# A second Strassen level in three products of a cross-attention and FFN kernel

## The chip, the cores and the metric

The kernel runs on one NeuronCore of a Trainium2 chip. The metric is the device time of one execution in microseconds (us). TensorE (PE in the profile) does the matmuls, VectorE (DVE) and ScalarE (ACT) the elementwise work, GpSimd (POOL) a few small steps, and SyncE (SP) issues all the transfers (DMAs) from one queue. A weight load of TensorE is a separate instruction, shown as the row PEld.

## The reference, cut to what matters

```
x = x + matmul(fake_quant(layernorm(x)), fake_quant(ctx))     # x: 2 x 1024 x 2048, ctx: 2 x 2048 x 2048
y = layernorm(x)
w = top-2 softmax weights of y @ W_router.T                   # 8 experts
lora = einsum(y @ lora_A, lora_B, w) * 2                      # rank 16 per expert
x = x + y @ W_base.T + b_base + lora                          # W_base: 2048 x 2048
```

All of it is in float32. `fake_quant` rounds to 256 levels, so the first GEMM is exact with float16 operands. The second GEMM, `y @ W_base.T`, needs more than float16: each operand is split into a high and a low float16 part, and a product takes three matmuls (low by high, high by low, high by high).

## The kernel before

The two batches run one after the other. For each, the first GEMM (`gemm1` for batch 0, `gemm1w` for batch 1), a second layer norm (`ln2`), the operands of the second GEMM (`y_prep`) and the second GEMM itself (`g2`) follow.

**Second GEMM.** It is done with the Winograd form of Strassen's method: 7 block products in place of 8. Rows are taken in NP = 4 pairs `p` of 128-row tiles, so a 2 by 2 block of the left matrix is (tile 2p, tile 2p+1) by (first, second half of the 2048 depth). `y_prep` makes seven left operands for each pair, `a11, a12, a22, s1, s2, s3, s4`, each by normalizing, adding or subtracting halves, splitting into high and low float16, and transposing by a DMA (`emit`, lines 1007 to 1023). They stay in SBUF. The output columns are two halves `cp` of 1024, one in each pass `f` = 0, 1. A pass has four groups `grp` (the table `GROUPS`), with the right operands made by `w_step` for each `k` of the HK = 8 blocks of the depth: loads of `W`, subtractions on DVE, a scaled high part (`hi`, ACT or DVE), the low part (`lo`, DVE, line 1211). A product is HK x NP x 3 = 96 matmuls of 512 columns (line 1406). At the last `k` of a group the LoRA matmuls (line 1423) and the evacuations follow: `x += scale * PSUM` on DVE (line 1435), 512 columns at a time. `put` stores finished output tiles.

Batch 0 in pass 1 stores ready right operands to DRAM (`store_w`, tiles `made`), and batch 1 in its pass 0, which has the same columns, loads them. The residual `x` tiles are stored (`spill`) before the second GEMM and loaded again for their pass (`reload`, tiles `xr`).

**Memory.** Nearly all of SBUF is one pool `u` of 49 slots, and PSUM has 8 banks. Bytes of the quantized values go through three buffers `byte`, which are handed out in a fixed rotation.

**Order.** Nothing is issued in the order of the code. Every step is a task with modelled durations, its reads and writes, and a priority (the time `t` at which TensorE is due to need it). `Plan.order` is a list scheduler with a model of the engines, of the DMA queue and of the slots. It fixes the order of every engine and of the SP queue when the kernel is built. On the chip each queue then runs strictly in that order: an instruction that waits holds all that is queued behind it on its engine.

## Time and profile before

| what | value |
|---|---|
| median of 3 runs | 910.81 us (910.04 to 912.2) |
| profiled execution, own time | 910.92 us |
| its span, first to last instruction | 909.1 us |
| PE busy, matmuls | 896.0 us, 4542 |
| DVE busy | 708.0 us |
| ACT busy | 388.7 us |
| DMA queue of SP | 240.23 MB, 86.8% of 16 engines' span |

Engine rows of the profile give busy time and its share of the span. The span is also cut into 40 slices of 22.7 us, each with one digit, the busy share in tenths. A group of instructions is listed with its source line, its operation, what it writes and reads, its count, its busy time, the mean ns of one, and the idle time of the engine just ahead of them with the releaser. Matmuls are pipelined: one of 512 columns is shown with 379 ns, but the next one starts after some 216 ns, so their pace is read from the distance of starts.

### The profile page before, as it was taken

Reading aid. Unit: us, or ns where it says so; the run is one execution under the profiler, and the core shown is the slowest. Engines: PE = TensorE matmul, PEld = TensorE weight load, DVE = VectorE, ACT = ScalarE, POOL = GpSimd, SP = SyncE. Lnnn points to the kernel's source line nnn. Section 1 sums busy time; section 2 is a strip of 40 time slices with the busy share of each in tenths; the row PEclk is TensorE's granted clock in tenths of the full one; section 3 lists DMA queues with packets and bytes.
Section 4 is the critical chain, followed back from the end, with each engine's and each line's share of the span. In section 5 each row is a group of like instructions: output and inputs, shape, how many; then the busy total and the mean of one; then the engine's idle time right before and its main releaser. Section 6 shows DMA issues by size and latency. Waiting matters only on the chain.

```text
span 909.1 us, 12499 instructions
## 1 busy us (share of the span) xinstructions
PE 896.0 (99%) x4542; PEld 432.4 (48%) x4542; DVE 708.0 (78%) x1305; ACT 388.7 (43%) x445; POOL 47.4 (5%) x199
## 2 busy tenths in 40 slices
PE   8899999999999999999999999999999999999998
PEld 6344446474444444444444444556444444444443
DVE  8989999999499966999889979999543363899131
ACT  4875976525144221323686776754100021324000
POOL 1014000000000000002540000000000000000000
PEclk9999999999999999999999999999999999999999
DMA  9999999998999999999999748999994169883021
GB/s 327 387 386 278 348 285 225 245 265 226 255 362 325 314 395 406 380 369 345 301 343 323 243 170 235 228 169 222 308 283 109 50 224 371 288 337 134 6 93 46
DMA packets 223917, 241.02 MB, mean 265 GB/s; under 512 B 146032, under 2 KB 158320, under 8 KB 223856
## 3 DMA queue, kind: packets, MB, share of 16 engines
q1 hardware_dynamic: 223856, 240.23, 86.8%
q8 instruction: 35, 0.57, 0.3%
q14 instruction: 26, 0.21, 0.1%
HBM read 163.65 MB, written 41.94 MB: 226 GB/s over the span
## 4 chain that ended last, share of the span: by engine, by line
PE 85%; DVE 9%; DMA 3%; issue 1%; SPq 1%; ACT 0%; DVEq 0%; ACTq 0%
PE X L1406 34%; PE Y L1406 27%; PE g L829 11%; PE gX L949 3%; PE ph L1067 3%; PE gY L949 2%; DVE x L858 2%; PE X L1423 2%; PE Y L1423 2%; PE ph L1071 1%; DMA x<-in_x_dram 1%; DVE byte L455 1%; DMA bs<-in_cx_dram 1%; DVE sm L478 1%; DVE bt L920 1%
## 5 line engine op out<-in xcount | busy, mean ns | idle before, releaser
L1406 PEld LDWEIGHTS <-y_s 128*128 128x128 f16 x1536 | 150.3, 98 | 181.0
L1406 PE MATMUL Y<-w,y_s 128*128 128x512 f16 x768 | 206.6, 379 | 0.0
L1406 PE MATMUL X<-w,y_s 128*128 128x512 f16 x768 | 206.3, 379 | 0.0
L1406 PE MATMUL X<-w,y_a 128*128 128x512 f16 x768 | 189.1, 379 | 0.2 <-DVE w L1211 0.2
L1406 PEld LDWEIGHTS <-y_a 128*128 128x128 f16 x1152 | 112.1, 98 | 132.6 <-issue 0.5
L829 PE MATMUL g<-b,at 128*128 128x512 f16 x512 | 112.5, 379 | 4.7 <-DVE b L469 3.6
L1406 PE MATMUL Y<-w,y_a 128*128 128x512 f16 x384 | 103.2, 379 | 0.0
L444 ACT ACTIVATE w<-wb,gW 128x1024 f16<-128x1024 f32 (+1 forms) x46 | 50.0, 1091 | 111.1 <-DVE wb L1282 32.9
L1435 DVE SCALAR_TENSOR_TENSOR xr<-X,uW,xr 128x512 f32<-128x512 f32 x64 | 46.8, 746 | 46.9 <-PE X L1423 25.7
L829 PEld LDWEIGHTS <-at 128*128 128x128 f16 x512 | 49.7, 98 | 64.3 <-issue 4.2
L1435 DVE SCALAR_TENSOR_TENSOR xr<-Y,uW,xr 128x512 f32<-128x512 f32 x42 | 31.1, 745 | 53.8 <-PE Y L1423 53.8
L1211 DVE SCALAR_TENSOR_TENSOR w<-wb,gW,w 128x1024 f16<-128x1024 f32 (+1 forms) x48 | 57.0, 1194 | 6.0 <-ACT w L444 5.9
L444 ACT ACTIVATE byte<-bs,sc,rec 128x1024 uint8<-128x1024 f32 x40 | 48.3, 1236 | 13.5 <-DMA bs<-in_cx_dram 8.6
L444 ACT ACTIVATE w<-wt,gW 128x1024 f16<-128x1024 f32 x15 | 17.0, 1145 | 78.5 <-DVE wt L1258 38.7
L478 DVE BATCH_NORM_STATS2 sm<-x 128x6 f32<-128x512 f32 x64 | 40.9, 683 | 5.5 <-ACT q L444 4.2
L877 ACT ACTIVATE byte<-x,sm 128x1024 uint8<-128x1024 f32 x32 | 36.4, 1139 | 10.4 <-DVE x L858 6.8
L444 ACT ACTIVATE nat_s<-yt_a 128x1024 f16<-128x1024 f32 x31 | 31.9, 1049 | 20.0 <-DVE yt_a L1026 14.7
L949 PEld LDWEIGHTS <-at 128*128 128x128 f16 x256 | 25.0, 98 | 29.8
L1026 DVE TENSOR_TENSOR yt_a<-yt_a,yt_a 128x1024 f32<-128x1024 f32 x32 | 38.7, 1221 | 0.0
L1018 DVE TENSOR_TENSOR nat_s<-yt_a,nat_s 128x1024 f16<-128x1024 f32 x32 | 38.2, 1224 | 0.0
L1067 PE MATMUL ph<-ar,y_a 128*128 128x272 f16 x192 | 35.7, 279 | 0.0
L1071 PE MATMUL ph<-ar,y_a 128*128 128x136 f16 x192 | 34.6, 223 | 0.0
(196 smaller groups left out, 1107.1 us busy)
## 6 DMA issues: line engine op xcount, KB each, us to landing
bs<-in_cx_dram SPq DMA_DIRECT2D x64, 512.0 KB, 10.5
wt<-in_wT_dram SPq DMA_DIRECT2D x64, 512.0 KB, 7.4
wn<-in_wT_dram SPq DMA_DIRECT2D x32, 512.0 KB, 9.1
x<-in_x_dram SPq DMA_DIRECT2D x30, 512.0 KB, 8.4
spill<-x SPq DMA_DIRECT2D x28, 512.0 KB, 4.4
xr<-spill SPq DMA_DIRECT2D x28, 512.0 KB, 8.5
wb<-in_wT_dram SPq DMA_DIRECT2D x24, 512.0 KB, 7.8
out_dram<-xr SPq DMA_DIRECT2D x24, 512.0 KB, 4.0
```

The lines of the kernel that those rows point to most:

```text
L444: nc.scalar.activation(o, i, AF.Copy if c is None else AF.Identity, scale=1.0 if a is None else a, bias=0.0 if c is None else c,)
L478: nc.vector.bn_stats(st[:, 2 * h + c], b.ap()[:, c * C : (c + 1) * C])
L829: nc.tensor.matmul(ps.ap(), aT.ap()[:, k, :], S["b", c, k // 4].ap()[:, k % 4, :], start=k == 0, stop=k == KT - 1,)
L877: nc.scalar.activation(low(sq), xb.ap(), AF.Square, bias=a[:, 22 + j : 23 + j], accum_out=a[:, 24 + 2 * j + h : 25 + 2 * j + h],)
L949: nc.tensor.matmul(ps.ap(), a()[:, 4 * h + k, :], w.ap()[:, k, :], start=fresh and h + k == 0, stop=h == 1 and k == 3, skip_group_check=True,)
L1018: lambda: nc.vector.tensor_tensor(n.ap()[:, 1], t.ap(), n.ap()[:, 0], ALU.subtract),
L1026: add("DVE", 1.22, lambda: nc.vector.tensor_tensor(dst.ap(), a.ap(), c.ap(), op), r=[a, c], w=[dst])
L1067: nc.tensor.matmul(ph.ap()[:, : 2 * AR], y[half].ap()[:, 0, k, :], ar[:, kr, :], start=kk == 0, stop=False,)
L1071: nc.tensor.matmul(ph.ap()[:, AR : 2 * AR], y[half].ap()[:, 1, k, :], ar[:, kr, :AR], start=False, stop=kk == KT - 1,)
L1211: lambda: nc.vector.scalar_tensor_tensor(w.ap()[:, 1, lo:up], src(), g, w.ap()[:, 0, lo:up], ALU.mult, ALU.subtract),
L1406: nc.tensor.matmul(ps.ap(), y.ap()[:, a, k, :], w.ap()[:, q, j * C : (j + 1) * C], start=k == 0 and fresh and i == 0, stop=k == HK - 1 and ...
L1435: nc.vector.scalar_tensor_tensor(xs, ps.ap(), uW[:, cp : cp + 1], xs, ALU.mult, ALU.add)
```

## The change

Three of the block products of batch 1 get a second Strassen level: `a22` in pass 0, `a22` and `a12` in pass 1 (`LEVEL2`). Such a product pairs the row pairs again (`q` = 0, 1 holds `p` = 2q and 2q+1) and cuts depth and columns in half again, so it becomes seven products of 4 blocks of depth, with 256 columns for each matmul (`quarters`). Two of its left operands come from `y_quarters`, which loads the spilled `x` again, normalizes it, combines quarters, and splits and transposes the results `q31` and `q24`; the third operand is the whole one that exists already.

For that, two more `x` tiles are spilled, and the `a12` operands of batch 1 are stored to DRAM in pass 0 (`y_out`) and loaded in pass 1 (`y_in`). A sum of blocks of `W` in float32 goes through DRAM too (`store_t4`): in batch 0, pass 0, group 1 stores its sum of three blocks, and group 3 loads it with the one block that is missing and subtracts once, where it loaded two whole rows and subtracted twice before; it stores the result, which is the right operand of `a22`, over it. Pass 1 stores that of the other column half in its group 2. Batch 1 loads these in quarters. The byte buffers are handed out as they come free, not in rotation, and the planner's time for a transpose on TensorE (`TMM`) is 0.08 in place of 0.12 us.

```
-TMM = 0.12
+TMM = 0.08
+MM2 = 0.1095
+LEVEL2 = {(0, 0): (), (0, 1): (), (1, 0): ("a22",), (1, 1): ("a22", "a12")}
+YOUT = ((), ("a12",))
+YQ = ((), ("a22", "a12"))
...
     def byte(name):
         def make():
-            ring = rings["byte"]
-            ring.append(ring.pop(0))
-            return ring[-1]
+            return rings["byte"].pop(0)
...
+    def y_out(S, b, p, o, when):
+        y = S["y", p, o]
+        d = Buf("dram", lambda: dram.tile([P, 2, HK, P], F16, name=f"yout_{o}_{b}_{p}"))
+        load(d, d.ap, y.ap, HD * 4, [d], r=[y], store=True, cap=when)
+        S["yout", p, o] = d
+
+    def y_in(S, b, p, o):
+        y = buf("u", [P, 2, HK, P], F16, f"yin_{o}_{b}_{p}")
+        d = S["yout", p, o]
+        load(y, y.ap, d.ap, HD * 4, [y], r=[d], far=YFAR)
+        S["y", p, o] = y
+
+    def y_quarters(S, b, q, o):
+        yt = []
+        j = int(o[1]) - 1
+        for p in (2 * q, 2 * q + 1):
+            s = S["s2", p]
+            d = S["spill", 2 * p + j, 1]
+            t = buf("u", [P, HD], F32, f"yq_{o}_{b}_{p}")
+            load(t, t.ap, d.ap, HD * 4, [t], r=[d])
+            affine(t.ap, t.ap, HD, [(s, [j])], [t], scale=lambda s=s: s.ap()[:, 10 + j : 11 + j],
+                   bias=lambda s=s: s.ap()[:, 12 + j : 13 + j])
+            yt.append(t)
...
+        comb(lambda: up(c), lambda: lo(c), lambda: up(c), ALU.add, [], c)
+        comb(lambda: lo(c), lambda: lo(a), lambda: lo(c), ALU.subtract, [a], c)
+        comb(lambda: lo(a), lambda: up(c), lambda: lo(a), ALU.subtract, [c], a)
+        comb(lambda: up(a), lambda: up(a), lambda: lo(a), ALU.subtract, [], a)
+        y_emit(S, b, 2 * q, o + "q31", c)
+        y_emit(S, b, 2 * q, o + "q24", a)
...
-                if h == b and p >= SPILL0:
+                if h == b and p >= SPILL0 and f"a{1 + i % 2}2" not in YQ[b]:
                     continue
...
+    def store_t4(k, cp, s, cap):
+        if cp not in whole_t4:
+            whole_t4[cp] = Buf(
+                "dram", lambda: dram.tile([P, HK, C], F32, name=f"t4_{cp}"), HK)
+        d = whole_t4[cp]
+        load(d, lambda: d.ap()[:, k], lambda: s.ap()[:, :C], C * 4, [(d, [k])], r=[s],
+             store=True, cap=cap)
...
+            elif not b:
+                s = buf("u", [P, HD], F32, f"wb_{n}")
+                d = whole_t4[cp]
...
+                load(s, lambda: s.ap()[:, C:], lambda: d.ap()[:, k], C * 4, [s], r=[(d, [k])], far=WFAR)
...
+        if grp == 2 and "a22" in LEVEL2[b, f]:
+            s = buf("u", [P, 2, C], F32, f"ws_{n}")
...
+    QUARTERS = (
+        ("b11", "", 0, 0), ("t1", "q31", 4, 0), ("t2", "q24", 0, 0), ("b22", "q24", 4, 0),
+        ("t3", "q31", 0, 0), ("b21", "", 4, 0), ("t4", "", 4, 1),
+    )
+
+    def quarters(S, b, f, cp, t, o):
+        g = gW[:, cp : cp + 1]
+        H2 = C // 2
+        raw, made_w = {}, {}
+        for h, n in ((0, 0), (0, 1), (1, 1), (1, 0)):
+            s = buf("u", [P, 4, H2], F32, f"wq{o}_{cp}_{h}{n}")
...
+            load(s, s.ap, src, HD * 4, [s], r=r, slow=SLOW_Q, far=WFAR)
+            raw[h, n] = s
...
+        split("b11", b11)
+        comb(t3, b22, b12)
+        comb(b12, b12, b11)
+        split("t1", b12)
+        t2 = b11
+        comb(t2, b22, b12)
+        split("t2", t2)
+        split("b22", b22)
+        split("t3", t3)
+        split("b21", b21)
+        comb(b21, b21, t2)
+        split("t4", b21)
...
+        for name, op, k0, side in QUARTERS:
+            w = made_w[name]
+            for q in range(NP // 2):
+                y = S["y", 2 * q + side, o + op]
...
+                def mm(ps=ps, col=col, fresh=fresh, y=y, w=w, k0=k0):
+                    for k in range(4):
+                        for i, (a, h) in enumerate(((1, 0), (0, 1), (0, 0))):
+                            nc.tensor.matmul(
+                                ps.ap()[:, col : col + H2], y.ap()[:, a, k0 + k, :],
+                                w.ap()[:, h, k * H2 : (k + 1) * H2],
...
+                add("PE", 12 * MM2, mm, r=[y, w], w=[ps], prio=t)
+                t += 12 * MM2
+                xP, xQ = top[2 * q], top[2 * q + 1]
+                if name == "b11":
+                    ev(ps, 0, H2, xP, 0)
+                elif name == "t1":
+                    ev(ps, 0, H2, xP, H2)
+                    ev(ps, 0, H2, xQ, H2)
...
+        for o in YQ[b]:
+            for q in range(NP // 2):
+                y_quarters(S, b, q, o)
...
+            for o in YOUT[b]:
+                for p in range(NP):
+                    if f:
+                        y_in(S, b, p, o)
+                    else:
+                        y_out(S, b, p, o, t + YO_T + 3.0 * p)
...
+                if grp == 3 and LEVEL2[b, f]:
+                    for o in LEVEL2[b, f]:
+                        t = quarters(S, b, f, cp, t, o)
+                    continue
...
         for task in order:
             task.fn(task.eng) if len(task.durs) > 1 else task.fn()
+            for b in task.bufs:
+                uses[b] -= 1
+                if b.tag in rings and not uses[b]:
+                    rings[b.tag].append(b.tile)
```

`split` is the high part (ACT or DVE) and the low part (DVE) of a right operand of 1024 columns; `comb` of `quarters` is one subtraction of 1024 columns on DVE; `ev` is an evacuation as before, of 256 or 512 columns. `y_emit` is `emit` of `y_prep` as a function of its own. The LoRA matmuls of the three products stay the same in number.

## The prediction

> **What bounds the kernel now.** I read the engine shares first, then the slices, the chain, the groups of instructions, the timeline, and at last windows of 25 us around the places that the change touches.
>
> ```profile
> span 909.1 us, 12499 instructions
> PE 896.0 (99%) x4542; PEld 432.4 (48%) x4542; DVE 708.0 (78%) x1305; ACT 388.7 (43%) x445; POOL 47.4 (5%) x199
> PE   8899999999999999999999999999999999999998
> DVE  8989999999499966999889979999543363899131
> ACT  4875976525144221323686776754100021324000
> PEclk9999999999999999999999999999999999999999
> DMA  9999999998999999999999748999994169883021
> PE 85%; DVE 9%; DMA 3%; issue 1%; SPq 1%; ACT 0%; DVEq 0%; ACTq 0%
> ```
>
> TensorE is the bound at full clock. DVE and the DMA queue are near full for the first two thirds, but from slice 29 on (659 us, the second GEMM of batch 1) DVE, ACT and DMA have room, except DVE in slices 34 to 36.
>
> ```profile
> L1406 PE MATMUL X<-w,y_a 128*128 128x512 f16 x768 | 189.1, 379 | 0.2 <-DVE w L1211 0.2
> L1435 DVE SCALAR_TENSOR_TENSOR xr<-X,uW,xr 128x512 f32<-128x512 f32 x64 | 46.8, 746 | 46.9 <-PE X L1423 25.7
> 882.56 18.78 PE X L1406 x87
> 7.82 5.62 PE L771 MATMUL warm<-ones 128*128 128x256 f16 x50
> 13.28 0.82 PE L780 MATMUL warm<-ones 128*128 128x256 f16 x6
> ```
>
> The second GEMM's matmuls wait for nothing (0.2 us idle in 768). The chain gives their pace: 18.78 / 87 = 215.9 ns for 512 columns, not the 379 ns shown. The timeline gives it for 256 columns: 50 warm-up matmuls, each with its own weight load, take 13.28 - 7.82 = 5.46 us, 109.2 ns each.
>
> ```profile
> 16.40:40.07 23.67, 17.43 (x116) 8.97 (x117) 22.66 (x69) 18.18 (x17) 0.00 (x0) 1.00 1.05 389
> 575.00:600.00 25.00, 25.00 (x127) 11.99 (x126) 22.34 (x65) 19.50 (x22) 0.00 (x0) 1.00 1.01 203
> 600.00:625.00 25.00, 25.00 (x194) 16.29 (x193) 25.00 (x27) 10.68 (x14) 0.00 (x0) 1.00 1.11 185
> 700.00:725.00 25.00, 25.00 (x117) 11.37 (x116) 6.51 (x10) 1.15 (x1) 0.00 (x0) 1.00 0.16 46
> 825.00:850.00 25.00, 25.00 (x117) 11.35 (x116) 19.33 (x26) 5.91 (x8) 0.00 (x0) 1.00 0.27 94
> 850.00:875.00 25.00, 25.00 (x117) 11.33 (x116) 0.92 (x2) 0.00 (x0) 0.00 (x0) 1.00 0.00 1
> ```
>
> Columns: window, its length, then busy time and count of PE, PEld, DVE, ACT and POOL, the clock, the DMA share, GB/s. TensorE loses 6.2 us (23.67 - 17.43) in the lead-in, where DVE is full; later it loses almost nothing.
>
> **TensorE, on the path.** A product of 96 matmuls of 512 columns becomes seven of 4 blocks x 2 pairs of pairs x 3 = 24 each, 168 matmuls of 256 columns. Three products: 288 x 215.9 = 62.2 us go and 504 x 109.2 = 55.0 us come: **-7.1 us**. The LoRA matmuls stay. Bounds: 504 x 107.9 (half the 512 pace) gives -7.8; 504 x 113 (5.62 / 50, the row's length with its tail) gives -5.2. I take the distance of starts.
>
> A rule of the Trainium skill speaks against this ("TensorE: Matmul & The Clock Gate", Part 3, The mechanism): a weight load runs beside a matmul in flight only where the two use different row groups. These all use the whole array, so each of the 216 additional loads would stand alone; at the row's 98 ns that adds 21.2 us and makes the sum +14 us. The rows decide otherwise: the warm-up matmuls' loads lie within the 109.2 ns.
>
> **DVE, beside TensorE if it is on time.** Added in batch 1, by rows of the same shapes: `y_quarters` 16 half-width combinations x 0.69 + 8 low parts x 1.22 = 20.8 us; `quarters` 12 subtractions x 1.22 + 21 low parts x 1.28 = 41.5 us; evacuations of 256 columns, 36 x 0.48 (between 0.30, the 136-column sum into `hf`, and 0.745 at 512 columns; the slope between 512 and 1024 columns, 0.535 us, gives 0.48). Removed: in pass 1 group 2, 8 x (1.22 + 0.69 + 1.28 - 0.69 - 0.75) = 14.0 us, group 3's 8 x 0.75 = 6.0 us; in batch 0, 8 x 1.22 = 9.8 us. With the 512-column evacuations, some 45 us net on 708. ACT gains 8 normalizations, 8 high parts and up to 21 scaled ones at 1.05 to 1.23 us, some 25 us net, in slices at 0 to 4 tenths.
>
> For `a22` of pass 0 the work fits: some 30 us of DVE into 660 to 725 us, where the windows show 6.5 to 15 busy of each 25. Its chain (four loads at the `xr` row's 8.5 us, four normalizations, the combinations, transposes at 4.4 us) is about 30 us; its loads stand in the queue right after the `hT` transposes, which the trace issues at 675 to 684 us, and TensorE needs the result at about 731 us. I cost it at nothing; without that cover, its last transposes would come straight onto the path, 4 x 4.4 = 18 us.
>
> Pass 1 is tight. In the changed DVE order, from the first evacuation of group 1 to the evacuation of `t2` of `a22`, I count 12 evacuations x 0.745, 4 bias additions x 1.22, 9 low parts x 1.28, one high part 0.78, 4 + 4 subtractions and low parts x 1.22, 8 combinations x 0.69 and 7 evacuations x 0.48: 44.8 us. Neighbours in the timeline start some 0.08 us before the end of the last, so 49 of them take 41 us. TensorE meanwhile does the rest of group 1 (7.0 us), group 2 (120 x 0.216 = 25.9) and eight steps of the level-2 product (8 x 1.31 = 10.5): 43.4 us, then `t3` needs that evacuation. Slack 2.4 us, with a low part among them that waits for a load (`b21` of `a12`) queued behind three pairs of transposes. Lower bound 0, upper bound a whole load behind time, 10.5 us (the `bs` row, the slowest of that size; its nearest in run length too, since 1 KB runs do not occur in the `wT` loads). I take **+0.5 us**.
>
> **SP queue and DMA.** 36 more issues: 8 loads of `x`, 2 spills, 4 + 4 transfers of `a12`, 16 transposes or 8 whole ones, 16 stores of the sum, less what the narrower loads save: about +7 MB of copies, +4 MB transposed. In batch 0 the stores stand beside loads made two lines shorter, at nothing; the cover is that TensorE has 8 blocks' operands queued ahead. The sensitive place is 550 to 625 us, with the DMA share above 1.0 and DVE full: two spills and four `y_out` stores are put among the transposes of the left operands. At 375 GB/s (slices full of loads show 360 to 400 on the page) each 512 KB is 1.4 us, 8.4 in all. Each store also waits on SP until the transposes of its tile have landed (4.2 us), and everything behind it in the queue waits too: the operands of pairs 2 and 3. Of those the trace issues the last at 587 to 592 us; with 4.2 us to landing they are there at 596, and by the count of matmuls TensorE first uses pair 3 at 597. Slack 1 to 3 us. The new order puts `wc` loads between a tile's transposes and its store, and moves two transfers (`wc`, `xr`) behind, so most of the hold is filled. Bounds 0 and 4 x 4.2 + 8.4 = 25 us; the order of TensorE's instructions in this stage is the same in both kernels, so the planner found no operand later than its neighbour: I take 0.
>
> The Trainium skill ("DMA: Bandwidth & Descriptors", Two DMAs through the same engine are not ordered) says why the hold cannot be dropped: the issuing engine has to wait for the first transfer's semaphore before a dependent one. No run here shows what happens otherwise.
>
> **Lead-in.** The new `TMM` and byte order move three of eight `at<-turn` copies from ACT to DVE (1.00 against 0.69 us) and four byte conversions from DVE to ACT (0.81 against 1.24): DVE -3.2 + 2.1 = -1.1 us where DVE is the bound, ACT +2.0 where it has 5.5 us free. Bounds -2.5 (that, and the 1.4 us that ACT waits there for a `byte` buffer gone) and +2 (ACT's gain on the path). I take half of DVE's relief: **-0.6 us**. The turn to batch 1 (475 to 530 us, DVE full, 1.25 us lost) is reordered a little too: 0, bounds -1 and +2.
>
> **Sum.** -7.1 + 0.5 - 0.6 = -7.2 us against the profiled execution's 910.92 (its span 909.1 and 1.8 around it), so 903.7. The median is 0.1 lower: **903.6 us**.
>
> **Rivals.**
> 1. *DVE or a late load takes a part back* in pass 1 (825 to 872 us) or at the lead-in. For: the slack of 2.4 us. Against: no such wait in batch 0's like stages. Price 2.5 to 5.5 us: 906 to 909 us.
> 2. *Slower: the `y_out` holds.* The queue waits for landed transposes at four stores, and pairs 1 to 3 come late, one after another. For: DMA above 1.0, slack 1 to 3 us. Against: the equal order of TensorE. Full price 16.8 of hold less 2 of slack, +14.8 - 7.1: 918.5 us. It decides once the holds exceed 7.1 + 2 + 1.8 = 11 us, that is three stores whose wait is exposed.
> 3. *No change*: the holds or the tail eat 5.3 to 9 us, 909.0 to 912.6 us.
> 4. *It does not do what it says*: 256 columns bound by the weight load. The load's 98 ns is below 109.2, and the mixed 272- and 136-column matmuls of `ph` start 8 pairs in 1.40 us, 87 ns each, so loads at a closer pace are hidden. Price if exposed as above; under 0.02, inside rival 2's chance.
>
> **Chances.** 0.64 for the forecast (901 to 906 us), 0.16 for rival 1, 0.07 for no change, 0.11 for slower, 0.02 for a lead-in better than its bound (below 901). A measurement can tell 0.2%, 1.8 us, from no change. Faster is 0.64 + 0.16 + 0.02 = 0.82. The range for 0.80 is 901 to 909 us; it takes in the bound of the matmuls (-5.2), of the lead-in and half that of the late load.
>
> **What would show it.** After: 504 matmuls of 256 columns whose starts are 109 ns apart; busy PE 7 us lower with its share still 99%; DVE about 45 us more; no PE idle with an evacuation or `y` as releaser. Wrong would be: PE idle near 585 to 600 us behind SP's `yout` (rival 2), near 866 to 872 us behind DVE (rival 1), or a pace near 200 ns at 256 columns.

## The result, and where the time went

The changed kernel takes 919.85 us (median of 7 runs, 916.4 to 923.6) against 911.34 us before (7 runs, 910.0 to 912.3): a ratio of 1.0091, 95% interval 1.0073 to 1.0110, so 8.3 us slower (6.7 to 10.0). The prediction said 903.6, range 901 to 909. It was wrong, and on the wrong side. One execution of `roundtrip_only`, a kernel shown below, took 3390.7 us against 913 to 918 in its other nine and is left out of its ratio.

The page of the changed kernel, the lines that answer to those of before:

```profile
span 918.1 us, 13150 instructions
PE 893.3 (97%) x4758; PEld 453.9 (49%) x4758; DVE 752.3 (82%) x1373; ACT 419.1 (46%) x471; POOL 47.8 (5%) x199
...
PE   8999999999989999999999999989899999999998
...
DVE  8989999999498665899898989889618597697983
...
DMA  9999999999999899999999649999999669773951
...
PE 29%; DVE 9%; DMA 3%; ACT 2%; issue 2%; SPq 0%; DVEq 0%; ACTq 0%
...
L1648 PE MATMUL X<-w,y_s 128*128 128x512 f16 x768 | 203.4, 381 | 5.3 <-DVE w L1265 2.7
...
L1648 PE MATMUL X<-w,y_a 128*128 128x512 f16 x576 | 146.4, 379 | 4.5 <-DMA y_a<-nat_a 3.2
```

DVE does 44 us more, as forecast. But the row of TensorE has digits of 8 in slices 12, 27 and 29, and the groups of the second GEMM's matmuls, of which one was shown with 0.2 us of waiting, now have 5.3 and 4.5. (TensorE's 29% of the chain that ended last can't be set beside the 85% of before: the shares add up to 45% here, so this chain was followed back over less than half of the span.)

The busy row of TensorE is too coarse to say where: a matmul of 512 columns is shown with 379 ns and the next one starts 216 ns after it, so a gap below 0.16 us can't be seen, and a longer one is shown too short. All matmuls are in both traces, so the loss can be counted by their starts. I take as a gap the distance of two starts less the first one's pace (0.4166 ns per column and 2.5 ns, 215.8 ns at 512 columns, the 216 of the prediction's chain). Over the whole kernel:

| us | before | after | difference |
|---|---|---|---|
| sum of the matmuls' paces | 890.8 | 883.8 | -7.0 |
| gaps, 0 to 50 us (lead-in) | 10.6 | 8.9 | -1.7 |
| gaps, 125 to 150 us (turn to the second GEMM, batch 0) | 0.6 | 1.6 | +1.0 |
| gaps, 250 to 350 us (batch 0, pass 0, groups 2 and 3) | 0.2 | 5.7 | +5.5 |
| gaps, 475 to 550 us (turn to batch 1) | 2.1 | 2.7 | +0.6 |
| gaps, 575 to 675 us (left operands of batch 1) | 0.0 | 8.1 | +8.0 |
| gaps, 725 to 750 us (start of `a22` of pass 0) | 0.0 | 2.5 | +2.5 |
| gaps elsewhere | 0.5 | 0.6 | +0.1 |
| all gaps | 14.0 | 30.0 | +16.0 |

The paces and the gaps make -7.0 + 16.0 = +9.0 us, the difference of the two spans (918.1 and 909.1). So the arithmetic did come out, to a tenth, and 16 us of waiting came on top of it: 5.5, 8.0 and 2.5 us at three places, each of which the prediction had put at nothing. The other differences cancel. In the timeline of the changed kernel, the matmuls behind the longest gaps (start, length, instructions, and in brackets the visible idle time and what ended it), and two steps of a second-level product:

```profile
255.64 0.59 PE L1648 MATMUL X<-w,y_s 128*128 128x512 f16 x2 [0.80 <-DVE w L1265]
...
262.67 0.59 PE L1648 MATMUL X<-w,y_s 128*128 128x512 f16 x2 [1.69 <-DVE w L1265]
...
605.79 0.82 PE L1648 MATMUL X<-w,y_a 128*128 128x512 f16 x3 [3.25 <-DMA y_a<-nat_a]
...
650.79 1.95 PE L1648 MATMUL X<-w,y_s 128*128 128x512 f16 x6 [2.61 <-DVE x L1677]
652.54 1.49 PE L1648 MATMUL Y<-w,y_s 128*128 128x512 f16 x3
...
744.39 1.49 PE L1487 MATMUL X_0a<-wqa_b,y_a 128*128 128x256 f16 x12 [0.99 <-DVE xr L1426]
...
877.30 1.47 PE L1487 MATMUL Y_0a<-wqa_t,y_a22q 128*128 128x256 f16 x12
878.61 1.47 PE L1487 MATMUL Y_1a<-wqa_t,y_a22q 128*128 128x256 f16 x12
```

The releasers are four different ones: a low part of `W` on DVE (255 and 263 us), a transposed tile (606), an evacuation behind other DVE work (651), an evacuation at the start of the quarters (744). The last two lines give the pace of the new matmuls: 12 in 1.31 us, 109.2 ns. Windows of the changed kernel (columns as before: busy time and count of PE, PEld, DVE, ACT, POOL, the clock, DMA share, GB/s):

```profile
250.00:275.00 25.00, 22.52 (x105) 10.02 (x104) 23.41 (x61) 10.49 (x17) 0.00 (x0) 1.00 1.00 331
...
600.00:625.00 25.00, 21.75 (x140) 12.19 (x139) 24.35 (x44) 13.05 (x13) 0.00 (x0) 1.00 1.10 214
650.00:675.00 25.00, 24.21 (x105) 10.69 (x105) 12.77 (x47) 1.31 (x2) 0.00 (x0) 0.93 1.10 287
...
825.00:850.00 25.00, 25.00 (x117) 11.37 (x116) 18.38 (x22) 8.72 (x8) 0.00 (x0) 1.00 0.33 110
850.00:875.00 25.00, 25.00 (x119) 11.43 (x117) 25.00 (x29) 13.39 (x13) 0.00 (x0) 1.00 0.94 247
```

The stage that the prediction thought tight, pass 1's tail at 825 to 875 us, has no idle time at all. At 650 to 675 the clock is 0.93: for 3.41 us behind the gap TensorE ran at half speed (three matmuls in 1.28 us at 652.54), which is 1.7 of the 8.1 us.

**What an idle count doesn't show.** The profile of before has no idle time of TensorE between 250 and 350 us, and the prediction took eight blocks' operands to be queued ahead there. They weren't. From the timeline of before, the low part (DVE, line 1211) of one block of group 2 and of one of group 3, and the first matmul of the block that needs each:

```profile
272.66 1.28 DVE L1211 SCALAR_TENSOR_TENSOR w<-wc,gW,w 128x1024 f16<-128x1024 f32 x1
...
276.05 0.81 PE L1406 MATMUL X<-w,y_s 128*128 128x512 f16 x3
...
305.83 0.75 DVE L1211 SCALAR_TENSOR_TENSOR w<-wb,gW,w 128x512 f16<-128x512 f32 x1
...
307.26 4.05 PE L1406 MATMUL X<-w,y_a 128*128 128x512 f16 x18
```

The first is done at 273.94 and wanted at 276.05, 2.1 us later; the second is done at 306.58 and wanted at 307.26, 0.7 us later. Paired over all blocks, this lead (from the end of the low part to the start of the block's first matmul) is, in us:

| second GEMM of batch 0 | before | after |
|---|---|---|
| pass 0, group 1 | 11.0 to 22.4 | 8.6 to 18.9 |
| pass 0, group 2, blocks 2 to 7 | 2.1 to 4.3 | -2.0 to 1.6 |
| pass 0, group 3, blocks 1 to 7 | 0.2 to 3.6 | -1.1 to 2.1 |
| pass 1, groups 0 to 3 | 3.0 to 37.5 | 8.2 to 36.8 |

(The block's first matmul reads the high part and the one 0.2 us behind it the low part, so a lead can be a little below 0 without a wait.) A lead of 0.2 us and one of 37 us look the same in an idle count. In the changed kernel group 1's leads are already 1 to 5 us shorter, before any gap of groups 2 and 3 appears.

### The profile page after: what moved, and what is told of

It is laid out like the page before. It is cut to its first block, busy times and chain, and to the rows that moved or that the text cites. A ratio compares the mean times of both kernels' runs of the same rounds, so it can differ in the third digit from the quotient of the medians.

```text
span 918.1 us, 13150 instructions
## 1 busy us (share of the span) xinstructions
PE 893.3 (97%) x4758; PEld 453.9 (49%) x4758; DVE 752.3 (82%) x1373; ACT 419.1 (46%) x471; POOL 47.8 (5%) x199
## 5 line engine op out<-in xcount | busy, mean ns | idle before, releaser
L1648 PE MATMUL X<-w,y_s 128*128 128x512 f16 x768 | 203.4, 381 | 5.3 <-DVE w L1265 2.7
L1648 PE MATMUL X<-w,y_a 128*128 128x512 f16 x576 | 146.4, 379 | 4.5 <-DMA y_a<-nat_a 3.2
L1648 PEld LDWEIGHTS <-y_a 128*128 128x128 f16 x864 | 83.8, 98 | 103.4 <-DMA y_a<-nat_a 3.7
L450 ACT ACTIVATE w<-wb,gW 128x1024 f16<-128x1024 f32 (+1 forms) x39 | 41.6, 1071 | 94.9 <-DVE wb L1350 41.0
L1648 PE MATMUL Y<-w,y_a 128*128 128x512 f16 x288 | 77.2, 379 | 0.0
L1677 DVE SCALAR_TENSOR_TENSOR xr<-X,uW,xr 128x512 f32<-128x512 f32 x53 | 38.6, 743 | 28.1 <-PE X L1648 27.6
L450 ACT ACTIVATE byte<-bs,sc,rec 128x1024 uint8<-128x1024 f32 x43 | 51.3, 1233 | 12.3 <-DMA bs<-in_cx_dram 7.9
L1265 DVE SCALAR_TENSOR_TENSOR w<-wb,gW,w 128x1024 f16<-128x1024 f32 (+1 forms) x40 | 46.7, 1173 | 11.4 <-ACT w L450 11.3
L883 ACT ACTIVATE byte<-x,sm 128x1024 uint8<-128x1024 f32 x32 | 36.5, 1140 | 10.7 <-DVE x L864 7.3
L450 ACT ACTIVATE yt_a<-x,sm 128x1024 f32<-128x1024 f32 x26 | 31.2, 1231 | 13.2 <-DVE sm L995 13.2
L1551 DVE TENSOR_TENSOR xr<-xr,bb 128x1024 f32<-128x1024 f32 x28 | 33.4, 1218 | 3.7 <-DMA bb<-in_bias_dram 3.7
```

The lines of the kernel that those rows point to most:

```text
L450: nc.scalar.activation(o, i, AF.Copy if c is None else AF.Identity, scale=1.0 if a is None else a, bias=0.0 if c is None else c,)
L883: nc.scalar.activation(low(sq), xb.ap(), AF.Square, bias=a[:, 22 + j : 23 + j], accum_out=a[:, 24 + 2 * j + h : 25 + 2 * j + h],)
L1265: lambda: nc.vector.scalar_tensor_tensor(w.ap()[:, 1, lo:up], src(), g, w.ap()[:, 0, lo:up], ALU.mult, ALU.subtract),
L1648: nc.tensor.matmul(ps.ap(), y.ap()[:, a, k, :], w.ap()[:, q, j * C : (j + 1) * C], start=k == 0 and fresh and i == 0, stop=k == HK - 1 and ...
L1677: nc.vector.scalar_tensor_tensor(xs, ps.ap(), uW[:, cp : cp + 1], xs, ALU.mult, ALU.add)
```

## The experiments

With no second level, the old lists and the old group 3, the changed code gives the order of before on every engine. So "one part alone" can be built from the constants, and the traces of such kernels have before's order up to the first instruction that a part adds. Gaps are from one profile each, ratios from 4 to 12 runs of the kernel against runs of before taken with them. Gaps of one order differ between profiles: seven kernels of the table (yout_alone, a12_pass1, a22_pass0, a22_a12, a22_yout and the two pass1_both) have before's order up to 379 us, and show 0.2 to 2.1 us at 250 to 350. A gap of up to 2 us in one profile says little there. All results at once, gaps in us by place:

| kernel | ratio to before, 95% | 0-50 | 125-150 | 250-350 | 475-550 | 575-675 | 725-775 | 825-900 |
|---|---|---|---|---|---|---|---|---|
| before | | 10.6 | 0.6 | 0.2 | 2.1 | 0 | 0 | 0 |
| changed | 1.0091 (1.0073-1.0110) | 8.9 | 1.6 | 5.7 | 2.7 | 8.1 | 2.5 | 0 |
| lists_only | 1.0013 (1.0000-1.0026) | 9.9 | 3.6 | 1.2 | 4.7 | 0 | 0 | 0 |
| roundtrip_only | 1.0036 (1.0020-1.0052) | 8.9 | 0.6 | 1.4 | 4.3 | 0.3 | 0 | 0 |
| no_roundtrip | 1.0085 (1.0068-1.0102) | 9.0 | 4.3 | 4.8 | 5.3 | 5.9 | 0.8 | 0 |
| no_yout | 1.0106 (1.0088-1.0125) | 9.1 | 3.0 | 3.2 | 2.9 | 0.7 | 8.3 | 0 |
| old_lists | 1.0071 (1.0051-1.0091) | 10.5 | 0.6 | 4.4 | 3.1 | 4.4 | 2.3 | 0 |
| a22_pass0 | 1.0063 (1.0047-1.0079) | 10.7 | 0.6 | 0.2 | 1.2 | 0.6 | 8.2 | 0 |
| a12_pass1 | 0.9971 (0.9958-0.9984) | 10.7 | 0.6 | 0.7 | 1.8 | 0 | 0 | 0 |
| a22_a12 | 1.0051 (1.0032-1.0069) | 11.3 | 0.6 | 0.8 | 2.5 | 0 | 8.9 | 0 |
| yout_alone | 1.0042 (1.0028-1.0056) | 10.3 | 0.6 | 0.2 | 1.7 | 4.0 | 0 | 0 |
| roundtrip_old | 1.0025 (1.0014-1.0036) | 10.7 | 0.6 | 1.2 | 4.3 | 0 | 0 | 0 |
| pass1_both | 0.9997 (0.9985-1.0009) | 11.5 | 0.6 | 0.4 | 1.7 | 0 | 0 | 5.9 |
| pass1_both_r | 0.9976 (0.9967-0.9984) | 11.0 | 0.6 | 2.1 | 1.1 | 0 | 0 | 2.5 |
| g3_store | 1.0095 (1.0074-1.0115) | 10.7 | 0.6 | 9.8 | 2.3 | 1.0 | 0 | 0 |
| t4_all | 1.0059 (1.0039-1.0079) | 10.6 | 0.6 | 4.2 | 3.3 | 0 | 0 | 0 |
| a22_yout | 1.0048 (1.0033-1.0062) | 10.7 | 0.6 | 0.9 | 1.1 | 3.5 | 3.6 | 0 |

### The lists and the sum's way through DRAM

**lists_only**: the changed kernel without level 2, and with batch 0's group 3 as before.

```
-LEVEL2 = {(0, 0): (), (0, 1): (), (1, 0): ("a22",), (1, 1): ("a22", "a12")}
-TABLE = {(0, 0): 0, (0, 1): 1, (1, 0): 0, (1, 1): 2}
-YOUT = ((), ("a12",))
-YQ = ((), ("a22", "a12"))
+LEVEL2 = {(0, 0): (), (0, 1): (), (1, 0): (), (1, 1): ()}
+TABLE = {(0, 0): 0, (0, 1): 1, (1, 0): 0, (1, 1): 1}
+YOUT = ((), ())
+YQ = ((), ())
...
-                if not b:
-                    store_t4(k, cp, s, t + PUT_W)
...
-            elif not b:
-                s = buf("u", [P, HD], F32, f"wb_{n}")
...
-                load(s, lambda: s.ap()[:, C:], lambda: d.ap()[:, k], C * 4, [s], r=[(d, [k])], far=WFAR)
```

> Only the handing out of byte buffers and TMM 0.08 are new; no second level, no sum through DRAM, no stored y tiles. Theory A (the sums' way through DRAM in batch 0 makes the weights late at 250 to 330 us): TensorE's gaps there stay near 0.2 us as before, and the kernel gains the lead-in's 1.5 to 2 us, less up to 1 us near 145 us: 0.5 to 2 us below before. Rival B (the new order from the lead-in on is what makes batch 0 late): some 5 us of gaps at 250 to 330 us, so 3 to 4 us above before.

It came out at 1.0013, no gain. The gap at 250 to 350 us is 1.2 (theory A's side), but the one at 125 to 150 us is 3.6. The waits of TensorE in that kernel at 130 to 152 us (us, times, longest):

```profile
PE ph L1113 <- DMA y_a<-nat_a: 1.8, 2, 1.4
PE ph L1117 <- DMA y_a<-nat_a: 0.9, 1, 0.9
```

The lead-in's gain is there in every kernel with the new lists (0.7 to 1.7 us). But the second GEMM begins when its first transposed tiles land, and in four of the five profiles with these lists the gain is lost again there: the gaps at 125 to 150 us are 1.6 to 4.3 us. In roundtrip_only they stay at 0.6. That the filled DMA queue sets when these tiles land is argued, not tested. The lists are worth +1.2 us (0 to 2.4), not -0.6.

**roundtrip_only**: as above, with the group 1 store and the group 3 load back in.

```
+                if not b:
+                    store_t4(k, cp, s, t + PUT_W)
...
+            elif not b:
...
+                load(s, lambda: s.ap()[:, C:], lambda: d.ap()[:, k], C * 4, [s], r=[(d, [k])], far=WFAR)
```

> As the kernel above, and batch 0's sum of four quarters is stored in group 1 and loaded again in group 3; still no second level. Theory A: group 2's low parts are ready 5 us later against TensorE than before (8 stores of 256 KB ahead of its loads in a full queue), the lead of 2 to 4 us is gone, and the gaps at 250 to 330 us are 3 to 6 us: that much above the kernel above. Rival B: no difference to the kernel above by more than 1 us.

1.0036, some 2 us above lists_only; the leads of blocks 2 to 7 of group 2 fell to between -0.6 and 1.6 us, from 0.7 to 2.8. But the gaps at 250 to 350 us are 1.4, not 3 to 6: theory A had the direction right and the size wrong. Up to 289 us every queue of this kernel has the same order as the changed kernel and as no_yout, and yet from 125 to 289 us the three have 1.9, 5.3 and 4.7 us of gaps. With leads near zero, differences between runs in when transfers land can turn into time.

**no_roundtrip**: the changed kernel, with batch 0's group 3 as before and the sum for batch 1 stored there alone.

```
-                if not b:
-                    store_t4(k, cp, s, t + PUT_W)
...
-            elif not b:
...
+                if not b and "a22" in LEVEL2[1, 1]:
+                    store_t4(k, cp, s, t + PUT_W)
```

> The changed kernel with batch 0's first pass computed from two full row loads as before: nothing stored in group 1, nothing loaded back in group 3; the sum that batch 1 needs is stored in group 3 alone. Theory A: the gaps at 250 to 290 us fall from 3.8 us to under 0.5 and the sum of gaps at 250 to 350 us from 5.7 to under 2.5: 3 to 5 us below the changed kernel, near 915 to 917. Rival B: gaps and time as in the changed kernel, 919 to 920.

Group 2's gaps are gone (0.0 at 250 to 300 us), as theory A wants, but group 3 has 4.8 us instead, and the time, forecast at 915 to 917 us, stayed at 920.7. The traffic was moved, not removed: a group 3 made of two whole rows, with a store behind each, costs as much as the way through DRAM did. That left group 3's stores to be looked at.

**roundtrip_old, g3_store, t4_all** add parts of this traffic alone to the order of before, with the old lists and no level 2. roundtrip_old has the store in group 1 and the load in group 3:

```
+                if not b:
+                    store_t4(k, cp, s, t + PUT_W)
...
+            elif not b:
...
+                load(s, lambda: s.ap()[:, C:], lambda: d.ap()[:, k], C * 4, [s], r=[(d, [k])], far=WFAR)
```

g3_store makes group 3 from two whole rows, as before, and stores its sum, which nobody reads here; t4_all has both.

```
+                if not b:
+                    store_t4(k, cp, s, t + PUT_W)
             hi(lambda: s.ap()[:, :m], 0, m, [s])
```

> The kernel before with one thing added: batch 0's first pass stores the sum of quarters in group 1 and loads it in group 3 in place of two half rows; old lists, TensorE's work unchanged, no second level. The prediction put this at nothing. Theory A (the low parts of group 2 stand only 2 to 4 us ahead of TensorE before, and the stores take about 2 us of that): leads near 0 in group 2, gaps of 1 to 4 us at 275 to 330 us, 1 to 3 us above before, 912 to 914. Rival B: none, 911.

> The kernel before with one thing added: in batch 0's first pass, group 3 stores its finished sum for batch 1 (8 stores of 256 KB); nothing reads it here. TensorE's work unchanged. Theory A (the low parts of group 3 stand 0.2 to 1.6 us ahead before, and each store takes about 0.7 us of a full queue between the loads): gaps of 2 to 5 us at 295 to 330 us, 2 to 5 us above before. Rival B (group 3's stores find room, the rest of the changed kernel's gaps there came from run-to-run differences in landing): within 1 us of before.

> The kernel before with both: the sum stored in group 1 and loaded in group 3, and the finished sum stored in group 3 again, the whole of the change's traffic in batch 0's first pass; no second level. Theory A: the sum of the two costs, some 4 to 6 us of gaps at 275 to 330 us, 4 to 6 us above before. Rival B: as with the sum of group 1 alone, 2 to 3 us above before.

They cost +2.3 us (1.3 to 3.3), +8.7 (6.7 to 10.5) and +5.4 (3.6 to 7.2). roundtrip_old is within its expectation by time, but only 1.2 us of gaps lie at 275 to 330 us, no more than before's order shows there from profile to profile. The rest is a longer gap at 490 us, behind which the clock was at half for 3.41 us, worth some 1.6 us. g3_store is far above its expectation: group 3, with 0.2 to 3.6 us of lead, then moves 1.25 MB for each block where it moved 1 MB. From its timeline:

```profile
306.25 0.58 PE L1638 MATMUL X<-w,y_a 128*128 128x512 f16 x1 [2.09 <-ACT w L452]
...
313.91 0.38 PE L1638 MATMUL X<-w,y_a 128*128 128x512 f16 x1 [0.98 <-ACT w L452]
315.60 2.72 PE L1638 MATMUL X<-w,y_a 128*128 128x512 f16 x8 [1.32 <-DVE w L1267]
```

The high and the low parts are late, and twice the clock falls to half behind it, which makes some 3 us of the 9.8. t4_all costs less than g3_store, and its leads in group 3 (blocks 1 to 7) are 1.7 to 7.6 us against -1.6 to 3.2; that the way through DRAM halves group 3's loads is the likely reason, not tested.

t4_all has the order of old_lists on every engine up to 383 us and nearly the same gaps at 250 to 350 us (4.2 and 4.4), so it shows the change's traffic with nothing else. With these leads its two longest gaps there don't wait for operands but for evacuations. The longest, and DVE ahead of it, from its timeline:

```profile
290.94 0.69 DVE L1303 TENSOR_TENSOR wb<-wb 128x512 f32<-128x512 f32 x1 [1.66 <-DMA wb<-t]
...
294.24 0.49 DVE L459 TENSOR_SCALAR w<-wb,gW 128x512 f16<-128x512 f32 x1 [1.29 <-DMA t<-wb]
...
295.43 0.74 DVE L1678 SCALAR_TENSOR_TENSOR x<-X,uW,x 128x512 f32<-128x512 f32 x1
...
296.23 1.02 PE L1649 MATMUL X<-w,y_a 128*128 128x512 f16 x4 [1.76 <-DVE x L1678]
```

DVE works in order here: it waits 1.66 us for a loaded sum and 1.29 us for a stored one to land, and the evacuation that TensorE needs comes behind both. Nor is it a matter of more bytes in all: from 200 to 330 us t4_all moves 39.0 MB and before 40.0. So the whole of the change's traffic in batch 0's first pass, put at nothing, costs 5.4 us by itself, in part by operands that come late and in part by DVE's waits for the sum's own transfers; how much by each isn't known. The rival, that group 3's stores find room, is out.

### The stored `a12` tiles

**no_yout**: `YOUT = ((), ("a12",))` becomes `YOUT = ((), ())` in the changed kernel.

> The changed kernel with the four a12 tiles of y kept in SBUF through both passes: no store of them at 565 to 603 us and no load at 854 to 876 us. If the stores and their waits hold the queue of transposes (rival 2 of the prediction): the 3.4 us gap at 606 us goes and the later ones of 650 us (2.8 us of waiting and 1.7 us of lower clock) shrink: 3 to 8 us below the changed kernel, 912 to 917. If the extra low parts, spills and DVE work make the left operands late: within 1.5 us of the changed kernel. Four fewer buffers for loads could also cost something in the first pass of batch 1; then gaps behind loaded weights at 610 to 740 us show it.

The gaps at 575 to 675 us go from 8.1 to 0.7, as expected, so the stores are their cause. But the time, forecast at 912 to 917 us, is 922.1, no better than the changed kernel's (1.0106). The four tiles stay in four of the 49 buffers, as the expectation's last sentence feared, and the start of the quarters loses 8.3 us in place of 2.5, in waits for a transposed quarter and for low parts; one stretch at half speed (743.7 us) is among them.

**yout_alone**: before's order with `YOUT = ((), ("a12",))` and nothing else.

> The kernel before with one thing added: the four a12 tiles of y are stored to DRAM in batch 1's first pass and loaded again in its last; no second level, old lists, TensorE's work unchanged. The prediction put the stores at nothing (0 to 25 us). If their holds make the left operands late as rival 2 has it: a gap of 3 us at 605 us behind a transposed tile and 1 to 4 us more near 650, none anywhere else, so 3 to 7 us above before, 914 to 918. If the gaps of the changed kernel there come from what level 2 adds besides (spills, low parts): within 1 us of before.

+3.8 us (2.6 to 5.1), with 4.0 us of gaps, all at 575 to 675 us. Its timeline shows the same two releasers as the changed kernel's:

```profile
597.28 0.82 PE L1638 MATMUL X<-w,y_a 128*128 128x512 f16 x3 [0.92 <-DMA y_a<-nat_a]
...
642.25 1.02 PE L1638 MATMUL X<-w,y_s 128*128 128x512 f16 x4 [2.61 <-DVE x L1667]
```

How they do it is not what rival 2 said. In the changed kernel all waits of the SP queue for a landed tile at such a store come to 1.2 us between 565 and 612 us, not four times 4.2. The line from the queue's waits there (us, times, longest):

```profile
SPq L431 <- DMA y_a<-nat_a: 1.2, 2, 0.8
```

The queue's timeline shows another way (start, length of the issue):

```profile
590.67 0.55 SPq L431 DMA_DIRECT2D spill<-x  x1
591.32 0.39 SPq L431 DMA_DIRECT2D yout_a<-y_a  x1
591.76 0.89 SPq L431 DMA_DIRECT2D wc<-in_wT_dram  x1
592.69 1.19 SPq L431 DMA_DIRECT2D xr<-spill  x1
593.98 6.06 SPq L440 DMA_TRANSPOSE y_a<-nat_a  x2
600.15 2.87 SPq L1017 DMA_TRANSPOSE y_a<-nat_a  x1
```

Four transfers of 512 KB stand straight ahead of the last pair's transposes, 2.1 MB, 5.6 us at the 375 GB/s of slices full of loads. Only one of them is a stored tile, but the order with the stores puts the four there. The transposes behind them take 2.0, 3.6 and 2.9 us to issue each, where they take 1.2 to 1.3 in before, and the last lands at 605.7. The `wc` loads among them also land later, and ACT, in order, waits 5.9 us for them there (before 1.5) with the left operands' work behind it, as its timeline shows:

```profile
598.84 1.15 ACT L450 ACTIVATE w<-wc,gW 128x1024 f16<-128x1024 f32 x1 [3.25 <-DMA wc<-in_wT_dram]
602.54 1.06 ACT L450 ACTIVATE nat_s<-yt_a 128x1024 f16<-128x1024 f32 x1 [2.55 <-DVE yt_a L1072]
```

The gap at 651 us is a late evacuation: on the chain of the changed kernel a transpose lands at 646.99, two low parts of left operands on DVE follow until 650.07, and only then comes the evacuation that frees TensorE's bank. That this delay is handed on from the one at 606 us is read from the profiles (both are there with the stores and absent without), not tested by itself.

### The lists undone, and level 2 piece by piece

**old_lists**: the changed kernel with `TMM = 0.12` and

```
-            return rings["byte"].pop(0)
+            ring = rings["byte"]
+            ring.append(ring.pop(0))
+            return ring[-1]
```

> The changed kernel with the old handing out of byte buffers in turn and TMM 0.12, so that the whole first GEMM of batch 0 runs in the order of before. If the new lists cost something behind the lead-in (the kernel with them alone came out at 1.0013 of before, with 0.6 to 4.3 us of gaps at 142 to 149 us in five profiles against 0.6 before): the gaps before 50 us are 10.5 us again, those at 125 to 150 us under 1, and the time is 1 to 2 us below the changed kernel, 918 to 919. If the lists do what the prediction says: about 1 us above it, 921.

The gaps at 0 to 50 us are 10.5 and those at 125 to 150 us 0.6 again, and the time is 1.0071 against 1.0091 with the lists. The intervals overlap, but with lists_only it is the second sign that the lists cost 1 to 2 us.

**a22_pass0, a12_pass1, a22_a12**: before's order with one or two products of level 2, no stored `y`, no sum through DRAM in batch 0's first pass. In this order:

```
+LEVEL2 = {(0, 0): (), (0, 1): (), (1, 0): ("a22",), (1, 1): ()}
+YQ = ((), ("a22",))
...
+LEVEL2 = {(0, 0): (), (0, 1): (), (1, 0): (), (1, 1): ("a12",)}
+YQ = ((), ("a12",))
...
+LEVEL2 = {(0, 0): (), (0, 1): (), (1, 0): ("a22",), (1, 1): ("a12",)}
+YQ = ((), ("a22", "a12"))
```

> The kernel before with one second-level product alone, a22 in the first pass of batch 1; old lists, no stored y tiles; the sum of quarters is stored in batch 0's second pass, where low parts are ready 15 to 25 us ahead. TensorE's own work falls by 168 x 109.2 - 96 x 215.9 = -2.4 us. Theory A (level 2 is a gain where its operands have cover, and the loss comes from places with under 4 us of it): no new gaps but those at the start of the quarters (2.5 us in the changed kernel, evacuations behind low parts on DVE), so 909 to 911.5. Theory B (level 2's own DVE and DMA work makes the left operands late between 570 and 660 us even without stored y tiles): gaps there of 2 us or more, 912 or above.

> The kernel before with one second-level product alone, a12 in the last pass of batch 1; old lists, no sum and no y tile through DRAM. Its operands are made at 700 to 860 us, where DMA and DVE have room. Theory A: no gap appears, and the whole -2.4 us comes out: 908.5 to 909.5, ratio about 0.997. Theory B: the two spills put among the transposes of batch 1 cost more than that: 911 or above, with gaps between 570 and 660 us.

> Both products of the two kernels above, nothing else of the change. Theory A: -4.8 us of TensorE work, less the start of the quarters: 906.5 to 909. Theory B: above 911. If the planner's order moves elsewhere, gaps away from 570 to 660 and 725 to 750 us show it.

a12_pass1 is the clean case: 908.59 us against 911.05, -2.6 us (-3.8 to -1.5) for a forecast of -2.4, with no new gap behind 575 us. It beats both kernels. From its page, and two of its windows:

```profile
PE 893.7 (99%) x4614; PEld 439.3 (48%) x4614; DVE 730.9 (81%) x1332; ACT 399.3 (44%) x452; POOL 48.5 (5%) x199
```

```profile
600.00:625.00 25.00, 25.00 (x194) 16.29 (x193) 25.00 (x27) 10.51 (x14) 0.00 (x0) 1.00 1.10 190
...
825.00:850.00 25.00, 25.00 (x117) 11.35 (x116) 25.00 (x32) 13.44 (x13) 0.00 (x0) 1.00 0.56 162
```

a22_pass0 is +5.7 us (4.3 to 7.2) where TensorE's own work falls by 2.4: 8.2 us of gaps stand at the start of the quarters, a stretch at half speed (737.6 us) included. Neither theory had that size; B's gaps at 570 to 660 us are only 0.6. The longest in its timeline, with the step on ACT that makes the high part of the late operand, and below them a line of the SP queue's waits at 680 to 745 us:

```profile
708.12 1.06 ACT L452 ACTIVATE nat_a22q<-yq_a 128x1024 f16<-128x1024 f32 x1 [12.30 <-PE Y L1638]
...
736.85 2.08 PE L1477 MATMUL Y_1a<-wqa_t,y_a22q 128*128 128x256 f16 x12 [3.51 <-DMA y_a22q<-nat_a22q]
```

```profile
SPq L433 <- PE Y L1638: 13.8, 3, 4.7
```

The loads of the sum's quarters wait 13.8 us for matmuls: they go into buffers that come free only as TensorE ends a block. The step on ACT waits 12.3 us for TensorE in the same way. a22_a12 is 4.6 us slower (2.9 to 6.3), the sum of the two (5.7 - 2.6 = 3.1) within its interval, with the gaps at the same place.

**a22_yout**: a22_pass0 with `YOUT = ((), ("a12",))`.

> The kernel before with the first pass's a22 in two levels, as in a22_pass0, and the four a12 tiles stored and loaded again, as in yout_alone; old lists, no sum through DRAM in the first pass of batch 0. TensorE's work falls by 2.4 us. If the late start of the quarters (8.2 us of gaps at 730 to 755 us in a22_pass0) is a lack of buffers: it falls to about 2.5 us, and the stores' own gaps at 597 to 650 us (some 4 us) come in its place: 914 to 917 in sum, no better than a22_pass0 by more than 2 us. If the late start is level 2's own DVE work, the 8 us stay, and the sum is 920.

915.97 us, and the gaps at 725 to 775 us fall from 8.2 to 3.6 while 3.5 us appear at 575 to 675. The step on ACT starts at 699.20 there, 8.9 us earlier and without such a wait; what is left of the gaps waits for evacuations on DVE. So the late start is a lack of buffers, and the stored tiles buy them at about what they save. The trade is even, and `a22` in pass 0 loses either way.

**pass1_both**: before's order with both products of pass 1; the sum for `a22` is stored by pass 1's own group 2.

```
+LEVEL2 = {(0, 0): (), (0, 1): (), (1, 0): (), (1, 1): ("a22", "a12")}
+YQ = ((), ("a22", "a12"))
...
+            if f:
+                top = load_wrow(k, cp, f"wt_{n}", far=WFAR)
+                bot = load_wrow(HK + k, cp, f"wb_{n}", far=WFAR)
...
+                hi(lambda: bot.ap()[:, C:], 0, C, [bot])
+                lo(lambda: bot.ap()[:, C:], 0, C, [bot])
+                store_t4(k, cp, bot, t - T4_T)
+                return
```

> The kernel before with both second-level products of the last pass, a22 and a12, and not that of the first; old lists, no stored y tiles, and the sum for a22 is made and stored in the last pass's own group 2, whose low parts stand 30 to 40 us ahead. TensorE's own work falls by 4.8 us. Theory A (the place has cover): 906 to 907. Rival: DVE has some 10 us more to do at 830 to 866 us than in the changed kernel, where 2 us of slack were counted, and the stored sum's loads come behind it; then gaps at 850 to 880 us take 2 to 8 us, 908 to 914.

No gain (0.9997): the rival. 5.9 us of gaps at 860 and 890 us, both behind DVE in its timeline, with some 1.6 us at half speed (889 to 893 us) among them:

```profile
860.34 1.47 PE L1446 MATMUL X<-lbs,hT 128*128 128x512 f16 x6 [1.02 <-DVE xr L1679]
...
889.87 1.44 PE L1489 MATMUL Y_0a<-wqa_t,y_a12q 128*128 128x256 f16 x6 [3.11 <-DVE wqa_t L1400]
```

**pass1_both_r**: the same with `("a12", "a22")`. In this order `a22`'s product is added to the banks of `a12` instead of those of `s3`, so its output is not what the reference asks for; the amount of work is the same, and only its time is read.

> As the kernel above with a12 first and a22 last, so that the stored sum has 18 us more. Theory A: the same 906 to 907. Rival: the gaps of the kernel above move to 870 to 900 us and shrink, to 0 to 3 us: 906 to 909.

0.9976: the gaps at 825 to 900 us shrink to 2.5. The second product of pass 1 gains about what DVE takes back, and nothing beyond a12_pass1.

## Why the prediction was wrong, step by step

- **TensorE's matmuls, -7.1 us: right.** The sum of paces fell by 7.0, 12 matmuls of 256 columns take 1.31 us, and a12_pass1 gains its third of that. The rule from the Trainium skill ("TensorE: Matmul & The Clock Gate", Part 3, The mechanism) that was weighed there, by which the new weight loads would stand alone, does not hold for these matmuls: 109.2 ns with a load each.
- **DVE, about +45 us: right** (+44.3). **The tail of pass 1, +0.5: right within its bounds**; it measured 0. pass1_both fits a slack of about 2 us: with some 10 us more of DVE work it was used up. (One slip in the bounds of the matmuls' term: 5.62 us over 50 are 112.4 ns, not 113, so its loose end is -5.5, not -5.2. Nothing rests on it.)
- **Batch 0's stores and loads "at nothing; the cover is that TensorE has 8 blocks' operands queued ahead": this step failed first.** The cover was never looked at. In that stage the leads are 0.2 to 4.3 us, and t4_all measures +5.4 us for the term: in part the low parts are late, in part the evacuations, behind DVE's waits for the sum's own transfers.
- **The stored tiles, "SP queue and DMA": 0 taken, +3.8 measured.** The bounds of 0 to 25 held it. The choice of the lower end rested on "the order of TensorE's instructions is the same in both kernels". It is, and says nothing: an order holds no times, and the same order ran with 0 and with 3.4 us of gap at that place. Rival 2 named the place and the releaser, but not the mechanism; its hold of 16.8 us is 1.2, and the delay is that of bytes ahead of transposes. That the result lies near rival 2's 918.5 us is a coincidence.
- **`a22` of pass 0 "costed at nothing": failed.** 2.5 us in the changed kernel, 8.2 without the buffers that the stored tiles free. The 30 us of chain and the free DVE time were counted, the free buffers were not, and the 18 us named for the case without cover were not let into the sum.
- **Lead-in, -0.6: the lead-in itself gained 1.7, but the term measures +1.2** (0 to 2.4). What the lead-in gains is lost again at 142 to 149 us in four of the five profiles with these lists and kept in roundtrip_only, and the runs of lists_only show no gain; why is not settled. **The turn to batch 1, 0**: +0.6 in the profile, inside its bounds.

The terms, four from runs of parts alone or from the matmuls and the 2.5 from the changed kernel's own profile, make -7.1 + 1.2 + 5.4 + 3.8 + 2.5 = +5.8 us, against +8.3 (6.7 to 10.0). The half-speed stretch at 652 us, which yout_alone did not have, is 1.7 of the remainder. The rest is not settled, and the terms need not add up: roundtrip_old and g3_store cost 2.3 and 8.7 us, both together 5.4.

The chances had the same fault as the sum. 0.82 for "faster" came from four zeros taken as one well-founded case, though each rested on its own unproved cover.

## What to carry to other kernels

Before a cost is put at nothing because TensorE doesn't wait, measure the lead of that stage, from the end of the operand's last producer to its first use: no idle time may mean 37 us of lead or 0.2. In two stages here with little in hand and a full DMA queue, added transfers came out in the time, whoever needed them: 2.1 MB of stores, 5.6 us of the queue, cost 3.8 us at the left operands of batch 1 and 8.7 in group 3 of batch 0's pass 0, where some 3 us of it were half speed. Look for a stage where the lead is long, ask too which engine will wait, in order, for the new transfers to land and what stands behind it, and take the parts of a change apart: of three second-level products here, the one that needed neither a stored sum nor a stored tile kept its whole gain, 2.6 us. The other two brought nothing on balance: `a22` of pass 0 costs 5.7 us by itself, and the second product of pass 1 gains nothing beyond the first.

## What was not expected of the hardware

**Half speed behind a short gap.** The record of the granted clock changes only in steps of 3.41 us. Over all 17 profiles, behind the lead-in, every such stretch with 2.15 us or more of TensorE idle, counted by the matmuls' starts as above, was followed by one at half speed (nine cases, 2.15 to 3.41 us; once a second one followed it), and none with 2.10 us or less at full speed was. It depends on how a gap lies across the steps: 2.77 us at 648 to 651 fell into one stretch (2.6 idle) and cost 1.7 us more, while 3.41 us at 602 to 606 was cut in two (1.4 and 2.0 idle) and cost nothing more. The Trainium skill ("TensorE: Matmul & The Clock Gate", HAM oscillation — how this bites in real kernels) gives as the rule that gaps should stay under about 3.4 us. The step of 3.41 us agrees; the bound is lower here.

**The same order, different gaps.** The three kernels with equal queues up to 289 us and the seven with before's order (0.2 to 2.1 us at 250 to 350) show that gaps are not fixed by the order alone; the changed kernel and no_yout, equal up to 563 us, have 5.7 and 3.2 us there. The times of the changed kernel spread by 7.3 us in 7 runs, those of before by 2.2 in the 7 beside them and by 4.2 in 34 later ones.
